# Between the layers of a graph network: the order of ScalarE's work over four chunks, and which queue issues the loads

## The chip, the cores and the metric

One core of a Trainium2 chip runs the whole kernel. The metric is the device time of one execution in microseconds (us); several runs are made and their median is given. Beside them one execution is recorded by the hardware profiler, and its trace is what the views below are read from.

The engines are called as in the profile: PE (TensorE matmul) with PEld (its weight loads), DVE (VectorE), ACT (ScalarE), POOL (GpSimd) and SP (SyncE). SP and ACT can both issue DMAs; "SPq" and "ACTq" mark that in the trace.

## The reference

Two layers of a graph network over 3125 nodes with 256 features and 50000 edges. Each layer adds a graph part and an attention part to `x`, and then a mixture-of-experts part:

```python
xn = _layernorm(x)
x = x + L0_gnn(xn, ...) + L0_mix(xn, ...)
x = x + L0_ffn(_layernorm(x), ...)          # shared expert + two of eight routed experts
xn = _layernorm(x)
x = x + L1_gnn(xn, ...) + L1_mix(xn, ...)   # attention over edges; Galerkin attention
x = x + L1_ffn(_layernorm(x), ...)

# L1_gnn, its start:
h_fwd = h @ W_forward.T                     # (3125, 64)
h_rev = h @ W_reverse.T
messages = h_fwd[src] * direction[:, 0:1] + h_rev[src] * direction[:, 1:2]
scores = messages @ attn.T                  # 4 heads
```

The change is in the step between the two layers: the two routed expert outputs of each node are added to `x`, `x` is normalised, transposed, and multiplied by the weights of `h_fwd` and `h_rev` and of the scores. The result is a table with one row of 136 values per node, from which the next step gathers by `src`.

## The kernel before

The 3125 nodes lie on 125 partitions in 25 tiles; `CHUNKS` groups the tiles as four chunks of four and three chunks of three. `self.x` stays in SBUF as 125 x 25 x 256 floats.

Layer 0's routed experts (`layer0_ffn`) scatter their outputs to `y2` in DRAM, two rows per node. When all scatters are done, `layer1_mix` calls `experts_in`, the function of the change. Its pools are closed when it ends; `layer1_mix` then takes new pools and fetches rows of `tab1` by indirect DMA on POOL (`gather`, L51), 391 of them in groups of eight, for the messages of layer 1. Layer 1's Galerkin attention is worked in between, and `layer1_ffn` follows.

`experts_in` runs in a block in which the order of PE, VectorE, ScalarE and SP is the order of the program (`manual_schedule`). In it:

- The loads: for each chunk, `y_in` (125 x 2 x 4 x 256) is read from `y2`, the first expert's half by SP, the second by ScalarE. `move` (L67) splits each half by partitions, 112 and 13, so there are 28 DMA issues, 14 on each of the two.
- `moments` (L1373 to L1378): VectorE adds both halves to `x`, takes `bn_stats` and `bn_aggr` of each tile; ScalarE takes the root of the variance.
- `table` (L1380 to L1400): VectorE takes the reciprocal (L1383) and minus mean times reciprocal (L1384). ScalarE writes the normalised rows (`ln_row`, L1388), one instruction per tile. PE transposes them (L1393) into PSUM (`ln_pt`, two halves of 128 features), and ScalarE copies them to `xT` (L1394). For each tile PE multiplies by `wcat` (`token_matmul`, L191) into a PSUM tile `pw`, and ScalarE copies it to `t1_st` (L1399), which the trace shows as `t_st`. SP stores the chunk to `tab1`, in two DMAs (L67), which the trace shows as `tab<-t_st`.
- The order: `moments` of a chunk, then `table` of the chunk before it.

Of the kernel before, what the change touches and what calls it, by code (L numbers as in the profile page):

```python
# [8 lines left out]
F32 = mybir.dt.float32  # L9
# [10 lines left out]
P = 125  # L20
NT = 25
CHUNKS = ((0, 4), (4, 4), (8, 4), (12, 4), (16, 3), (19, 3), (22, 3))
# [40 lines left out]
def move(queue, out, in_):  # L63


    for s in (slice(0, 112), slice(112, P)):
        queue.dma_start(out[s], in_[s])  # L67
# [7 lines left out]
def rows_of(table):  # L75
    return table.rearrange("(t p) d -> p t d", p=P)
# [12 lines left out]
class Kernel:  # L89
# [1265 lines left out]
    def experts_in(self, pool, psum, psum_m, xT):  # L1355

        nc, W = self.nc, 68
        mv = pool.tile([P, NT, 2], F32, name="ln_mv2")  # L1360
        rs = pool.tile([P, 2, NT], F32, name="ln_rs2")
        y2 = self.y2[:2 * N].rearrange("(i t p) d -> p i t d", i=2, p=P)
        loads = []
        for t0, n in CHUNKS:
            r = pool.tile([P, 2, 4, D], F32, name="y_in", bufs=len(CHUNKS))
            for i, queue in enumerate((nc.sync, nc.scalar)):
                move(queue, r[:, i, :n, :], y2[:, i, t0:t0 + n, :])
            loads.append(r)

        def moments(r, t0, n):  # L1370
            s = slice(t0, t0 + n)
            for i in range(2):
                nc.vector.tensor_add(self.x[:, s, :], self.x[:, s, :], r[:, i, :n, :])  # L1373
            st = pool.tile([P, 4, 6], F32, name="ln_st2", bufs=2)
            for t in range(t0, t0 + n):
                nc.vector.bn_stats(st[:, t - t0, :], self.x[:, t, :])
                nc.vector.bn_aggr(mv[:, t, :], st[:, t - t0, :])
            nc.scalar.activation(rs[:, 0, s], mv[:, s, 1], AF.Sqrt, bias=self.eps[:P])  # L1378

        def table(t0, n):  # L1380
            s = slice(t0, t0 + n)

            nc.vector.reciprocal(rs[:, 0, s], rs[:, 0, s])  # L1383
            nc.vector.scalar_tensor_tensor(rs[:, 1, s], mv[:, s, 0], -1.0, rs[:, 0, s], op0=OP.mult, op1=OP.mult)  # L1384
            row = pool.tile([P, 4, D], F32, name="ln_row2", bufs=2)
            for i in range(n):
                t = t0 + i
                nc.scalar.activation(row[:, i, :], self.x[:, t, :], AF.Identity, bias=rs[:, 1, t:t + 1],  # L1388
                                     scale=rs[:, 0, t:t + 1])
            for k in range(2):  # L1390
                pt = psum.tile([128, 4, P], F32, name="ln_pt")
                for i in range(n):
                    nc.tensor.transpose(pt[:, i, :], row[:, i, k * 128:(k + 1) * 128], self.ident[:P, :P])  # L1393
                nc.scalar.copy(xT[:, k, t0 * P:(t0 + n) * P], pt[:, :n, :].rearrange("p a b -> p (a b)"))  # L1394
            st = pool.tile([P, 4, 2 * W], F32, name="t1_st", bufs=2)
            for i in range(n):
                pm = psum_m.tile([P, 4, 65], F32, name="pw").rearrange("p h c -> p (h c)")[:, :2 * W]
                self.token_matmul(pm, xT, t0 + i, self.wcat)
                nc.scalar.copy(st[:, i, :], pm)  # L1399
            move(nc.sync, rows_of(self.tab1)[:, t0:t0 + n, :], st[:, :n, :])  # L1400

        before = None
        for r, chunk in zip(loads, CHUNKS):
            moments(r, *chunk)
            if before is not None:
                table(*before)
            before = chunk
        table(*before)

    def layer1_any_order(self):  # L1410

# [572 lines left out]
```

## Time and profile before

| What | us |
|---|---|
| median of 3 runs (2798.62 to 2800.9) | 2798.82 |
| the profiled execution, its own time | 2800.13 |
| its span in the trace | 2798.4 |
| first load of `y_in` issued (SP) | 1537.50 |
| first addition of `y_in` to `x` starts | 1544.11 |
| last of ScalarE's load issues begins | 1560.1 |
| first root begins | 1561.88 |
| last store of `tab1` issued | 1610.6 |
| first gather from `tab1` begins | 1613.86 |

Over the whole span PE is busy for 79%, POOL 59%, DVE 54% and ACT 19%. These shares say little on a stage of some 75 us out of 2800: the views that count are those restricted to the stage. In the table of busy time by stretch, each row gives the stretch, its length, the busy time of each engine with the number of its instructions in brackets, the granted PE clock (1.00 is full speed), the mean busy share of the DMA engines (it can exceed 1[...]) and GB/s. In a timeline, each row has the start, the length from the first start to the last end of a run of like instructions, what they are and how many; in square brackets stands how long the engine was idle before them, and what released it.

### The profile page before, as it was taken

The page shows a single profiled execution, that of the slowest core. Times are in us where ns is not written, and L with a number is a line of the kernel's source. Part 1 is how long each engine was busy: PE and PEld are TensorE (multiplying, and loading weights), DVE is VectorE, ACT ScalarE, POOL GpSimd, SP SyncE. Part 2 cuts the span into 40 slices and gives each one's busy share as a digit, 9 for nine tenths or more (in the row PEclk, how much of TensorE's full clock was granted, in tenths as well). Part 3 has the DMA queues.
Part 4 walks back from the last instruction along what each step waited for, and adds up shares of the span by engine and source line. Part 5 has one row for each costly group of instructions (what it writes and reads, how often), then busy time and mean ns, then how long its engine had stood idle before and what let it go on. Part 6 is the DMA issues. An engine that isn't in the chain of part 4 may idle for free. (4 is left out here: it accounts for less than half of the span.)

```text
span 2798.4 us, 26658 instructions
## 1 busy us (share of the span) xinstructions
PE 2201.9 (79%) x9047; PEld 1657.6 (59%) x9047; DVE 1508.4 (54%) x3589; ACT 544.0 (19%) x1116; POOL 1659.7 (59%) x1486
## 2 busy tenths in 40 slices
PE   1761659999976997999999549998667756999963
PEld 1551547876763665888887436665555644666642
DVE  7976499455568701222111459988658861222226
ACT  2320000000011111222222424444000020132213
POOL 4888788773002804666665077777747606777751
PEclk9955769999977998999999669999888867999976
DMA  8920433224400304455553421111211121112252
GB/s 296 382 102 14 116 90 90 62 52 90 114 32 21 81 5 160 163 184 181 183 189 107 113 70 49 47 47 47 57 32 41 39 66 40 25 40 53 53 109 70
DMA packets 175937, 259.79 MB, mean 93 GB/s; under 512 B 53839, under 2 KB 140857, under 8 KB 172402
## 3 DMA queue, kind: packets, MB, share of 16 engines
q1 hardware_dynamic: 114273, 198.43, 23.1%
q0 software_dynamic: 52288, 47.17, 7.3%
q10 hardware_dynamic: 9222, 12.30, 1.4%
q8 instruction: 76, 1.25, 0.2%
q14 instruction: 78, 0.64, 0.1%
HBM read 173.99 MB, written 83.69 MB: 92 GB/s over the span
## 5 line engine op out<-in xcount | busy, mean ns | idle before, releaser
L58 POOL DMA_INDIRECT adj<-ch_sum,ch_place x391 | 505.9, 1294 | 152.8 <-issue 109.7
L51 POOL DMA_INDIRECT g<-tab,t_src x391 | 459.0, 1174 | 152.6 <-issue 110.8
L58 POOL DMA_INDIRECT sorted<-s_rows,pos x256 | 245.1, 957 | 181.9 <-DVE s_rows L1059 112.4
L460 PE MATMUL psum<-sup,adjT 125*125 125x256 f32 x1250 | 294.1, 395 | 50.9 <-DMA adjT<-adj 39.6
L1288 PE MATMUL pw<-v,hot 128*125 128x260 f32 x1244 | 318.1, 417 | 0.0
L51 POOL DMA_INDIRECT G<-tabg,g_src x256 | 252.6, 987 | 80.2 <-issue 71.2
L460 PEld LDWEIGHTS psum<-sup,adjT 125*125 125x125 f32 x1250 | 241.8, 195 | 92.7 <-DMA adjT<-adj 36.4
L1288 PEld LDWEIGHTS pw<-v,hot 128*125 128x125 f32 x1244 | 252.2, 206 | 47.0
L866 PE MATMUL ph<-xs,w 128*128 128x256 f32 x960 | 219.3, 387 | 22.9 <-issue 20.5
L866 PEld LDWEIGHTS ph<-xs,w 128*128 128x128 f32 x960 | 183.2, 193 | 58.2 <-issue 31.0
L894 PE MATMUL py<-w,h 128*128 128x256 f32 x960 | 216.7, 379 | 0.0
L1700 PE MATMUL fpy<-fw,fh 128*125 128x256 f32 x800 | 186.2, 389 | 32.9 <-DVE y L1702 28.0
L1700 PEld LDWEIGHTS fpy<-fw,fh 128*125 128x125 f32 x800 | 152.6, 192 | 70.4 <-DVE y L1702 29.2
L894 PEld LDWEIGHTS py<-w,h 128*128 128x128 f32 x960 | 180.1, 190 | 23.3
L868 ACT ACTIVATE h<-ph,b 128x256 f32<-128x256 f32 x240 | 113.4, 473 | 361.4 <-PE ph L866 330.1
L1692 PE MATMUL fph<-xT,fw 128*128 128x500 f32 (+1 forms) x448 | 175.8, 542 | 0.2 <-DMA fw<-in_L_ffn_W_dram 0.2
L1034 PE MATMUL pctx<-s_mv,s_ro 128*128 128x256 f32 x512 | 155.4, 415 | 1.9 <-DVE s_mv L1033 1.9
L58 POOL DMA_INDIRECT slots<-rows,abi x50 | 74.3, 1485 | 100.2 <-DVE r_cum L948 85.3
L897 DVE TENSOR_SCALAR yo<-py,own 128x256 f32<-128x256 f32 x60 | 27.8, 481 | 190.8 <-PE py L894 190.8
L1694 ACT ACTIVATE fh<-fph,cols 128x500 f32<-128x500 f32 (+1 forms) x112 | 70.2, 632 | 298.0 <-PE fph L1692 264.0
L1692 PEld LDWEIGHTS fph<-xT,fw 128*128 128x128 f32 x448 | 85.4, 192 | 72.0 <-issue 49.4
L463 DVE TENSOR_TENSOR x<-x,psum 125x512 f32<-125x512 f32 (+1 forms) x104 | 68.9, 664 | 109.4 <-PE psum L460 109.3
(535 smaller groups left out, 3355.0 us busy)
## 6 DMA issues: line engine op xcount, KB each, us to landing
adjT<-adj SPq DMA_DIRECT2D x25, 1367.2 KB
adj<-zero SPq DMA_DIRECT2D x22, 1536.0 KB
w<-in_L_ffn_W1p_dram SPq DMA_DIRECT2D x30, 1024.0 KB
w<-in_L_ffn_W2p_dram SPq DMA_DIRECT2D x30, 1024.0 KB
slots<-empty SPq DMA_DIRECT2D x1, 8448.0 KB
srow<-slots SPq DMA_DIRECT2D x30, 264.0 KB
adj<-ch_sum,ch_place POOLq DMA_INDIRECT x391
g<-tab,t_src POOLq DMA_INDIRECT x391
```

The source lines that it names most:

```text
L51: nc.gpsimd.indirect_dma_start(out=out, out_offset=None, in_=table, in_offset=bass.IndirectOffsetOnAxis(ap=idx, axis=0))
L58: return nc.gpsimd.indirect_dma_start(out=table, out_offset=bass.IndirectOffsetOnAxis(ap=idx, axis=0), in_=rows, in_offset=None, **kw)
L460: nc.tensor.matmul(pm[:, i, :], mats[b][:, (a0 + i) * P:(a0 + i + 1) * P], sup[:, b, :], start=(b == b0), stop=(b == b0 + n - 1))
L463: nc.vector.tensor_add(xs, xs, pm[:, :m, :])
L866: nc.tensor.matmul(ph, w1[:, k, f * 128:(f + 1) * 128], xs[:, k, :], start=(k == 0), stop=(k == 1))
L868: nc.scalar.activation(h[:, f, :], ph, AF.Gelu, bias=b1[:, f:f + 1])
L894: nc.tensor.matmul(py, h[:, f, i * 128:(i + 1) * 128], w2[:, f, :], start=(f == 0), stop=(f == FC - 1))
L1034: nc.tensor.matmul(p1, ro[:, f - f0, :], mv, **st)
L1288: nc.tensor.matmul(pw.rearrange("p h c -> p (h c)"), hot[:, i - i0, :], v[:, i, :, :].rearrange("p h c -> p (h c)"), start=(i == i0), stop ...
L1692: nc.tensor.matmul(ph[:, :n * P], w1[:, k, f * 128:(f + 1) * 128], xT[:, k, t0 * P:(t0 + n) * P], start=(k == 0), stop=(k == 1))
L1694: nc.scalar.activation(hs[:, f, :n * P], ph[:, :n * P], AF.Gelu, bias=self.col("L1_ffn_b1", ei * FC + f))
L1700: nc.tensor.matmul(py, hs[:, f, i * P:(i + 1) * P], w2[:, f, :], start=(f == 0), stop=(f == FC - 1))
```

## The change

All 28 loads are issued by SP. `table` is split in three: `rows` (reciprocal, and the rows on ScalarE), `turned` (transposes on PE and their copies) and `table` (products and their copies, and the store). In turn c the program takes the moments and the root of chunk c, the rows of c-1, the transposes of c-2 and the products of c-3; three turns without moments end it. Two tiles of products share one PSUM tile (2 x 256 floats, of which 2 x 136 are used) and are copied by one instruction; a chunk of three tiles has a pair and a single. `t1_st` has three buffers in place of two; the PSUM pool of `pw` has four buffers, as before.

```diff
         for t0, n in CHUNKS:
             r = pool.tile([P, 2, 4, D], F32, name="y_in", bufs=len(CHUNKS))
-            for i, queue in enumerate((nc.sync, nc.scalar)):
-                move(queue, r[:, i, :n, :], y2[:, i, t0:t0 + n, :])
+            for i in range(2):
+                move(nc.sync, r[:, i, :n, :], y2[:, i, t0:t0 + n, :])
             loads.append(r)
...
-        def table(t0, n):
+        def rows(t0, n):
             s = slice(t0, t0 + n)
 
             nc.vector.reciprocal(rs[:, 0, s], rs[:, 0, s])
...
                 nc.scalar.activation(row[:, i, :], self.x[:, t, :], AF.Identity, bias=rs[:, 1, t:t + 1],
                                      scale=rs[:, 0, t:t + 1])
+            return row
+
+        def turned(row, t0, n):
             for k in range(2):
                 pt = psum.tile([128, 4, P], F32, name="ln_pt")
                 for i in range(n):
                     nc.tensor.transpose(pt[:, i, :], row[:, i, k * 128:(k + 1) * 128], self.ident[:P, :P])
                 nc.scalar.copy(xT[:, k, t0 * P:(t0 + n) * P], pt[:, :n, :].rearrange("p a b -> p (a b)"))
-            st = pool.tile([P, 4, 2 * W], F32, name="t1_st", bufs=2)
-            for i in range(n):
-                pm = psum_m.tile([P, 4, 65], F32, name="pw").rearrange("p h c -> p (h c)")[:, :2 * W]
-                self.token_matmul(pm, xT, t0 + i, self.wcat)
-                nc.scalar.copy(st[:, i, :], pm)
+
+        def table(t0, n):
+            st = pool.tile([P, 4, 2 * W], F32, name="t1_st", bufs=3)
+            for i in range(0, n, 2):
+                m = min(2, n - i)
+                pm = psum_m.tile([P, 2, 256], F32, name="pw")[:, :, :2 * W]
+                for j in range(m):
+                    self.token_matmul(pm[:, j, :], xT, t0 + i + j, self.wcat)
+                nc.scalar.copy(st[:, i:i + m, :], pm[:, :m, :])
             move(nc.sync, rows_of(self.tab1)[:, t0:t0 + n, :], st[:, :n, :])
 
-        before = None
-        for r, chunk in zip(loads, CHUNKS):
-            moments(r, *chunk)
-            if before is not None:
-                table(*before)
-            before = chunk
-        table(*before)
+
+        ready = {}
+        for c in range(len(CHUNKS) + 3):
+            if c < len(CHUNKS):
+                moments(loads[c], *CHUNKS[c])
+            if 0 <= c - 1 < len(CHUNKS):
+                ready[c - 1] = rows(*CHUNKS[c - 1])
+            if 0 <= c - 2 < len(CHUNKS):
+                turned(ready.pop(c - 2), *CHUNKS[c - 2])
+            if 0 <= c - 3 < len(CHUNKS):
+                table(*CHUNKS[c - 3])
```

## The prediction

> **What bounds the kernel now.** The diff touches one function, `experts_in`, so I first ask where in the span it lies and what it holds up. The list of waits for 1530 to 1615 us answers both (engine, tile or line waited at, releaser: us in total, times, longest).
>
> ```profile
> POOL late L1196 <- DMA tab<-t_st: 77.1, 1, 77.1
> ACT L1378 <- DMA y_in<-y: 39.1, 1, 39.1
> ...
> DVE ln_rs L1383 <- ACT ln_rs L1378: 23.0, 5, 8.7
> ...
> ACT t_st L1399 <- PE pw L191: 16.8, 25, 1.0
> ...
> DVE top L1204 <- DMA tab<-t_st: 13.9, 1, 13.9
> ```
>
> GpSimd does nothing for 77.1 us until the last store of `tab1` has landed; VectorE waits for the same store. PE, ScalarE and the SP queue start nothing of the next stage before it either (the timeline has the first next-stage load at 1612.73, the first gather at 1613.86). So this stage is serial with the rest: it runs from the first load, 1537.5, to 1612.8, and its 75.3 us are on the path. Nothing else is in flight, so a shorter stage moves all that follows. (The page's printed chain of waits starts only at 2269 us, which is why I use the waits.)
>
> Next the table of busy time by stretch shows what limits each part.
>
> ```profile
> core 0: us, PE busy (x) PEld busy (x) DVE busy (x) ACT busy (x) POOL busy (x), PEclk, DMA share, GB/s
> 1537.50:1544.10 6.60, 0.00 (x0) 0.00 (x0) 0.00 (x0) 0.00 (x0) 0.00 (x0) 0.50 0.86 204
> 1544.10:1553.50 9.40, 0.00 (x0) 0.00 (x0) 8.98 (x20) 0.00 (x0) 0.00 (x0) 0.50 1.12 255
> 1553.50:1562.20 8.70, 0.00 (x0) 0.00 (x0) 0.00 (x1) 1.60 (x3) 0.00 (x0) 0.50 1.07 254
> 1562.20:1576.00 13.80, 10.84 (x42) 8.15 (x43) 13.11 (x34) 7.97 (x19) 0.00 (x0) 0.62 0.21 54
> 1576.00:1610.20 34.20, 26.41 (x110) 20.52 (x109) 8.24 (x25) 19.38 (x51) 0.00 (x0) 0.70 0.14 36
> ```
>
> Three things: VectorE is full for two chunks and then stands still for 8.7 us; afterwards no engine is full, though each is often waited for; and loads fill the DMA engines at about 255 GB/s until 1564. The ScalarE timeline (start, us, what, idle before) gives the cause of the stop and the rhythm after it.
>
> ```profile
> 1537.74 22.82 ACTq L67 DMA_DIRECT2D y_in<-y  x14
> 1560.58 1.28 ACT L1378 ACT_TABLE_LOAD   x1 [39.05 <-DMA y_in<-y]
> 1561.88 0.48 ACT L1378 ACTIVATE ln_rs<-ln_mv,eps 125x4 f32<-125x4 f32 x2
> ...
> 1570.66 2.06 ACT L1388 ACTIVATE ln_row<-x,ln_rs 125x256 f32<-125x256 f32 x4
> 1573.14 1.05 ACT L1394 COPY xT<-ln_pt 128x500 f32<-128x500 f32 x2 [0.42 <-PE ln_pt L1393]
> 1575.09 0.27 ACT L1399 COPY t_st<-pw 125x136 f32<-125x136 f32 x1 [0.90 <-PE pw L191]
> 1576.00 0.27 ACT L1399 COPY t_st<-pw 125x136 f32<-125x136 f32 x1 [0.63 <-PE pw L191]
> 1576.91 0.27 ACT L1399 COPY t_st<-pw 125x136 f32<-125x136 f32 x1 [0.64 <-PE pw L191]
> 1577.81 0.27 ACT L1399 COPY t_st<-pw 125x136 f32<-125x136 f32 x1 [0.63 <-PE pw L191]
> 1577.98 0.30 ACT L1378 ACTIVATE ln_rs<-ln_mv,eps 125x4 f32<-125x4 f32 x1
> ```
>
> ScalarE issues 14 of the 28 loads, and the later ones go out only as earlier ones land: the last at about 1560.2. Both roots stood ready behind them (1548.8 and 1553.5). Then a chunk is one serial round: rows, PE transposes, copy, PE products, four copies each after its product, and only then the next root: 7.5 us for four tiles (1570.5 to 1578.0), 6.0 to 7.1 for three.
>
> **What the Trainium skill says.** "DMA: Bandwidth & Descriptors", Issuing engines are not separate DMA queues: issuing from several engines saves only issue time, the 16 DMA engines are shared. The trace agrees as far as it goes: the late layer's `yback` loads, of the same 1 KB rows and on SP alone (with a store and a few gathers beside them), run at 205 to 268 GB/s between 2702 and 2716 us. "TensorE: Matmul & The Clock Gate", Part 1: the clock is half until a window of about 3.4 us was busy, and falls back after idling. The trace agrees: PEclk is 0.50 before, 1.00 at 1572 to 1574 after PE was full from 1564 to 1570, and 0.57 in the next two microseconds although PE had been a half busy between. "ScalarE: Activation LUTs", What ACT_TABLE_LOAD costs: a copy without pointer operands takes 186 ns and 0.833 ns per element. The rows here are slightly below (272 ns at 136 columns, 299 by the page).
>
> **The change, part by part.** Durations are from this trace.
>
> *Loads.* ScalarE loses 14 issues; SP gains 14 of 0.3 to 0.4 us. SP's 28 issues (some 10 us) fit in the 22 us over which the transfers meter them out; eight were in flight over both queues at first (four on each), and the SP-only `yback` loads got about eight out too. Chunk 0's four issues are now in series, so it may land 0.4 us later. Behind them SP has the stores of `tab1`, the first needed near 1568, after the last load issue near 1560: nothing is delayed. The root of chunk 0 no longer waits for 1560.5, so VectorE's 8.7 us stop goes.
>
> *VectorE is then the pacer.* Its order is unchanged. Moments take 4.66 us for four tiles (1562.50 to 1567.16) and 3.68 for three; reciprocal and product 0.28 a chunk. From 1544.1: 4 x 4.66 + 3 x 3.68 + 6 x 0.28 = 31.4, so the last moments end at 1575.5. Loads keep ahead: chunks 1 to 6 are 5.38 MB, at 205 GB/s 26.2 us, thus in by 1570.3, before VectorE reaches the last chunk at 1571.8.
>
> *ScalarE, staggered.* In one turn it does root c, rows c-1, copies c-2, table copies c-3, so PE has a turn to get ready. Pitches: root 0.2, rows 4 x 0.52, transposed copies 2 x 0.53. The 25 single copies (0.272 each) become 14, of which 11 have two tiles: from 272 ns at 136, 474 at 375 and 578 at 500 columns I estimate 0.39 us at 272 (0.41 by the page), pitch 0.32. Four tiles: 0.2 + 2.1 + 1.06 + 0.64 = 4.0 us a turn, below VectorE's 4.94. Added wait: a root waits for its moments with the rows and copies of three older chunks queued behind it, and PE's products and SP's stores wait for those. It costs nothing while VectorE paces the turns; its price is the three turns that remain at the end.
>
> *PE.* A cold tile of products takes 0.90 us (spacing of the copies), a warm one 0.46 (1591.65 to 1592.11); a transpose 0.24 or 0.12 when rows are ready. Four tiles: 5.5 us cold, 2.8 warm. Cold it is slower than VectorE, then full, and full is what makes it warm; so I expect alternation, with little lag.
>
> *Tail, warm.* At 1575.5 ScalarE owes root 6 (0.3), rows 5 (1.57), copies 4 (0.87), table 3 (0.64), rows 6 (1.57), copies 5 (0.87), table 4 (0.52), copies 6 (0.87), table 5 (0.52): 7.7 us; then the last product and copy, 1.2: about 1584.4. *Cold throughout*, PE sets the end: from the first transpose of chunk 1 (1559.4), 21 tiles x 2 x 0.24 + 25 x 0.90 = 32.6, plus about 1.2 of waits and the last copy: 1593.2. I take a quarter of the way, 1586.6, plus 0.4 for the first landing: 1587.0. Today the last copy ends at 1610.2; store and landing after it (2.6 us) stay. **Gain 23.2 us.**
>
> *Third `t1_st` buffer, four pair-wide PSUM tiles:* nothing; a pair is copied only when both its tiles are done, which the one-turn delay covers. Without that cover it is one tile, 0.46 to 0.90 us, per pair.
>
> **Sum.** The profiled execution took 2800.13 us (span 2798.4), 1.3 above the median of 2798.82. The gain is a difference within the trace and carries over to the median: 2798.8 - 23.2 = 2775.6.
>
> **Rivals.**
> *PE stays cold* (0.15). For it: before, PE is at half clock most of the time. Against: it then is 100% busy. End 1593.6, gain 16.6: 2782.
> *One queue is slower* (0.10): if loads only reach 150 GB/s, 5.38 MB take 35.9 us, the last chunk lands at 1580.4, its moments end at 1584.1, tail 9: 1593.1 and up; at 120 GB/s 1601.9. Some 2782 to 2791. Against: the `yback` rate.
> *The gain is given back* (0.04): gathers after 1613.9 take another course, or the clock of later PE stages falls otherwise; within 0.2% of today, 2793 to 2804. Against: all engines start the next stage together from idle.
> *Slower* (0.05): one SP ring starves the DMA engines. The point from which it decides: last landing past 1597.5 (1610.2 less 9 and 3.7), that is 5.38 MB in 53.0 us, 101 GB/s. At 90 GB/s the last copy falls at 1617.0: 2805.6. For it: twice the issues share one queue, and each waits for an earlier transfer.
> That the order is not kept is no case: this block is scheduled by hand for PE, VectorE, ScalarE and SP.
>
> **How the numbers follow.** My forecast has 0.66; its own span is 2771 (warm, first landing not late, 1 us of run spread) to 2780. The range goes on through the cold case and the milder slow-queue case: 2769 to 2787. A measurement of this kernel tells about 0.2% (5.6 us) from no change. Faster: 0.66 + 0.15 + 0.10 = 0.91; same 0.04; slower 0.05.
>
> **What would show it.** Right: the first root near 1550, no stop of VectorE above 1 us between 1544 and 1575, rows of chunk 0 before 1555, 14 table copies of which 11 are near 0.39 us, last copy at 1584 to 1590, first gather 23 us earlier. Wrong: y_in below 200 GB/s, VectorE waiting for loads, PEclk at 0.50 through 1590 (the cold case), or a message stage longer than its 1613.9 to 2265.7.

## The result, and the profile after

The changed kernel takes **2772.03 us** (median of 6 runs, 2770.59 to 2775.72) against 2798.75 (6 runs of the kernel before): 26.7 us less, ratio **0.9909**, 95% interval 0.9896 to 0.9923. The forecast was 2775.6, with a gain of 23.2. The profiled execution of the changed kernel took 2771.34 us, with a span of 2769.6.

The two spans differ by 28.8 us. Cut at the first load issue of the stage, the start of GpSimd's next work (when the last store of `tab1` has landed) and the first load of the last layer, they compare so:

| Part of the span | before, us | after, us | difference |
|---|---|---|---|
| up to the first `y_in` issue | 1537.5 | 1535.4 | -2.1 |
| the stage of the change | 75.3 | 47.3 | **-28.0** |
| messages of layer 1 | 652.9 | 653.9 | +1.0 |
| last layer | 532.7 | 532.9 | +0.2 |

The 2.1 us ahead of the stage are not the change's, since the two kernels are the same up to there. The stage gain was passed on but for 1.2 us, which leaves 26.8, close to the 26.7 of the medians. The waits of the stage (engine, tile and line waited at, releaser: us in total, times, longest) show what went:

```profile
POOL late L1196 <- DMA tab<-t_st: 49.1, 1, 49.1
ACT L1378 <- DVE ln_mv L1377: 26.1, 1, 26.1
PE ln_pt L1396 <- ACT ln_row L1388: 22.2, 8, 19.1
...
ACT ln_rs L1378 <- DVE ln_mv L1377: 7.6, 4, 2.9
...
ACT t_st L1406 <- PE pw L191: 0.7, 1, 0.7
```

ScalarE's first root now waits for VectorE's moments and no longer for loads; VectorE's 23.0 us of waiting for roots is gone from the list; ScalarE's 16.8 us of waiting for products has become 0.7. The stretches (length, busy time of each engine, PE clock, DMA share, GB/s):

```profile
1535.44:1541.89 6.45, 0.00 (x0) 0.00 (x0) 1.23 (x2) 0.00 (x0) 0.00 (x0) 0.50 0.87 212
1541.89:1550.31 8.42, 0.00 (x0) 0.00 (x0) 8.01 (x22) 1.84 (x3) 0.00 (x0) 0.50 1.12 246
1550.31:1561.90 11.59, 8.64 (x31) 6.28 (x32) 11.08 (x26) 7.33 (x17) 0.00 (x0) 0.50 1.05 254
1561.90:1571.40 9.50, 8.74 (x66) 7.59 (x66) 8.95 (x28) 9.06 (x22) 0.00 (x0) 0.98 0.24 62
1571.40:1580.20 8.80, 7.89 (x57) 6.42 (x56) 0.59 (x5) 7.89 (x21) 0.00 (x0) 1.00 0.38 99
```

VectorE is full from 1541.9 to the last moments at 1571.4 (28.0 of 29.5 us). In the tail after that PE and ScalarE are both busy for 7.9 of 8.8 us. PE's clock is at full speed from just after 1562. The ScalarE timeline has the turn that was intended, here with the rows of chunk 3, the copies of 2, and the table copies of 1 with no wait in between:

```profile
1563.75 0.30 ACT L1378 ACTIVATE ln_rs<-ln_mv,eps 125x3 f32<-125x3 f32 x1
1564.07 2.08 ACT L1388 ACTIVATE ln_row<-x,ln_rs 125x256 f32<-125x256 f32 x4
1566.05 1.03 ACT L1397 COPY xT<-ln_pt 128x500 f32<-128x500 f32 x2
1566.97 0.67 ACT L1406 COPY t_st<-pw 125x272 f32<-125x272 f32 x2
1567.61 0.30 ACT L1378 ACTIVATE ln_rs<-ln_mv,eps 125x3 f32<-125x3 f32 x1
```

### The profile page after: what moved, and what is told of

Read it like the earlier page. It is cut to its first block, busy times and chain, and to the rows that moved or that the text cites. A ratio compares the mean times of both kernels' runs of the same rounds, so it can differ in the third digit from the quotient of the medians.

```text
span 2769.6 us, 26648 instructions
## 1 busy us (share of the span) xinstructions
PE 2190.7 (79%) x9047; PEld 1650.7 (60%) x9047; DVE 1506.8 (54%) x3589; ACT 541.6 (20%) x1105; POOL 1661.3 (60%) x1486
```

## The experiments

They ran on other chips of the same kind, where the kernel before takes 3176 to 3206 us. The changed kernel has a stage of 47.8 us on such a chip (`e11`, in the last group), so for it the excess lies outside the stage. Each kernel is therefore read by the length of its stage in its own trace, one execution each (first `y_in` issue to GpSimd's first instruction after the last landing), and by the ratio of its time to that of the kernel before on the same chip. The kernel before left no trace there: its 75.3 us are from the first chip. `e5`, `e6`, `e7` and `e9` ran once each, so only their stages are used.

**The parts, singly and in pairs.** `e1` is the kernel before with this edit alone:

```diff
-            for i, queue in enumerate((nc.sync, nc.scalar)):
-                move(queue, r[:, i, :n, :], y2[:, i, t0:t0 + n, :])
+            for i in range(2):
+                move(nc.sync, r[:, i, :n, :], y2[:, i, t0:t0 + n, :])
```

> The kernel before with only the first part of the change: SP issues all 28 loads; one round per chunk and single copies stay. The stage (first load issue to the landing of the last table store, seen at GpSimd's first instruction) was 75.3 us before and 47.3 after. Theory A (a root stood behind ScalarE's own blocked issues, worth VectorE's 8.7 us stop, and chunk 0 lands earlier from one queue, 1.3): stage 65.3 us (64 to 67), time about 2789. Rival B (issuing queues only save issue time, so the order of ScalarE's work makes the gain): stage 74 to 75, time 2798. Rival C (one queue feeds slower): y_in below 230 GB/s and VectorE waiting for loads after chunk 0.

Measured: stage 62.3 us, 13.0 less; ratio 0.9975 (0.9945 to 1.0005), so whole runs alone do not tell this gain. Theory A has the cause right, but the stage lies below its range: ScalarE's waits for products fell too, from 16.8 to 13.9 us. Rival C falls: VectorE does not wait for loads after chunk 0.

`e2` is the changed kernel with the two queues put back:

```diff
-            for i in range(2):
-                move(nc.sync, r[:, i, :n, :], y2[:, i, t0:t0 + n, :])
+            for i, queue in enumerate((nc.sync, nc.scalar)):
+                move(queue, r[:, i, :n, :], y2[:, i, t0:t0 + n, :])
```

> The changed kernel with the loads as before, half of them issued by ScalarE; the staggered turns and the pair copies stay. Theory A: the roots stand behind the issues until about 23 us into the stage, VectorE stops again for 8 to 9 us, then 2 x 4.9 + 3 x 3.9 us of moments follow, 8.8 of tail and 2.6 of landing: stage 57.8 us (57 to 60), time about 2782. Rival B (the order alone carries the gain): stage 47 to 49, time 2772.

Measured: stage 58.6 us, ratio 0.995 (0.9925 to 0.9975). The ScalarE timeline shows the stop again: issuing for 23.8 us, then the table load, then two roots at once.

```profile
1798.52 23.80 ACTq L67 DMA_DIRECT2D y_in<-y  x14
1822.36 1.28 ACT L1378 ACT_TABLE_LOAD   x1 [40.04 <-DMA y_in<-y]
1823.65 0.48 ACT L1378 ACTIVATE ln_rs<-ln_mv,eps 125x4 f32<-125x4 f32 x2
```

This is in the range of theory A. Rival B falls with both runs: the loads are worth 13.0 us without the new order and 11.3 with it, the order 16.7 without the loads and 15.0 with them.

`e3` keeps loads and turns, but copies each tile of products alone:

```diff
-            for i in range(0, n, 2):
-                m = min(2, n - i)
-                pm = psum_m.tile([P, 2, 256], F32, name="pw")[:, :, :2 * W]
...
+            for i in range(n):
+                pm = psum_m.tile([P, 4, 65], F32, name="pw").rearrange("p h c -> p (h c)")[:, :2 * W]
+                self.token_matmul(pm, xT, t0 + i, self.wcat)
+                nc.scalar.copy(st[:, i, :], pm)
```

> The changed kernel with one copy per tile of products and the old PSUM tile, so 25 copies of 136 columns in place of 14; loads on SP and staggered turns stay. Theory A: the pairs save ScalarE 25 x 0.18 less 14 x 0.3, some 1 us over the stage, and only that of the last three turns is on the path: stage 47.3 to 48.5. Rival D (with four single PSUM tiles ScalarE waits for each product again, as before): 0.2 to 0.5 us for each of 25 tiles, stage 52 to 58.

Measured: stage 47.6 us, ratio 0.9922 (0.9894 to 0.995). ScalarE waits 0.6 us for products in all. Pairs are not what took the waits away; the delay is.

`e4` is `e1` with the pairs:

```diff
-            for i in range(n):
-                pm = psum_m.tile([P, 4, 65], F32, name="pw").rearrange("p h c -> p (h c)")[:, :2 * W]
-                self.token_matmul(pm, xT, t0 + i, self.wcat)
-                nc.scalar.copy(st[:, i, :], pm)
+            for i in range(0, n, 2):
+                m = min(2, n - i)
+                pm = psum_m.tile([P, 2, 256], F32, name="pw")[:, :, :2 * W]
...
```

> The kernel before with the loads on SP and the pair copies, but one serial round per chunk. Theory A: in a serial round a pair waits for both of its products and saves one copy; stage as with the loads alone, within 1 us (64 to 67). Rival D: the pairs are what takes the waits for products away: stage 55 to 60.

Measured: stage 66.0 us, ratio 1.0 (0.998 to 1.002). Rival D falls. Theory A's 64 to 67 holds the number, but not its claim: it is **3.7 us more** than with the loads alone, not within 1. Without the delay a pair waits for its second product, as its waits show (14 copies, 18.6 us, against 25 copies and 13.9 in `e1`), in the timeline mostly 1.8 us at the first pair:

```profile
1809.99 0.39 ACT L1401 COPY t_st<-pw 125x272 f32<-125x272 f32 x1 [1.81 <-PE pw L191]
```

PE's clock is lower too: its mean is 0.67 over the second half of the rounds, against 0.86 in `e1`, and for the same 150 instructions PE is busy for 38.4 us in place of 33.6. How much of the 3.7 us is the clock's, these runs do not tell; it could be all of it.

**Issuing, or being blocked.** `e5` gives ScalarE 4 of the 28 issues:

```diff
             for i in range(2):
-                move(nc.sync, r[:, i, :n, :], y2[:, i, t0:t0 + n, :])
+                queue = nc.scalar if i and t0 < 8 else nc.sync
+                move(queue, r[:, i, :n, :], y2[:, i, t0:t0 + n, :])
```

> The changed kernel, but ScalarE issues the second half of the first two chunks (4 of 28 issues), SP the rest. These four go out while nothing has to land first. Theory A (it is the blocked issues that cost, not the issuing): ScalarE is free about 2 us into the stage, no stop of VectorE between chunks. The first half of chunk 0 shares the engines with its second half again, so VectorE starts at 6.5 us in place of 4.5 and the stage is 48.6 (48 to 49.5). Rival (any issue by ScalarE delays the roots): stage 55 or more. Rival (the early landing has nothing to do with the second queue): VectorE starts at 4.5, stage 47.3.

Measured: stage 49.1 us. VectorE begins 6.9 us after the first issue (1789.10) and then waits for no root. ScalarE's four issues are over 2.3 us after it, and the first root waits for its moments alone:

```profile
1789.34 2.10 ACTq L67 DMA_DIRECT2D y_in<-y  x4
...
1800.81 0.30 ACT L1379 ACTIVATE ln_rs<-ln_mv,eps 125x4 f32<-125x4 f32 x1 [8.06 <-DVE ln_mv L1378]
```

So four issues by ScalarE are cheap; in the kernel before, standing behind issues that wait for earlier landings is what cost. And the second queue does delay the first half of chunk 0: VectorE began after 4.5 us in the changed kernel and after 4.7 in `e11`. The stage is 1.3 to 1.8 us longer.

**Is PE the pacer?** `e6` works each product twice:

```diff
-                    self.token_matmul(pm[:, j, :], xT, t0 + i + j, self.wcat)
+                    for _ in range(2):
+                        self.token_matmul(pm[:, j, :], xT, t0 + i + j, self.wcat)
```

> The changed kernel with each tile of products worked twice into the same PSUM region, the second overwriting the first: 25 x 0.48 = 12 us more of warm PE. Theory A (VectorE paces until its last moments, PE is warm with 40% to spare, the tail is exposed): PE then needs 4.8 us of 4.9 in a turn of four, the turns stay, and only the products left at the last moments (13 tiles) show, 6.2 us: stage 53 to 56. Rival (PE paces the stage): the full 12 us and more, stage 59 to 61, with VectorE stopping.

Measured: stage 55.0 us, within the range of theory A. The last moments end 36.5 us after the first issue; in the changed kernel they do at 36.0, and at 36.4 in `e11`. VectorE stops only after them, for 2.0 us. So of the 12 us of added products none to speak of show while VectorE paced, and 7.2 us in the tail and landing (18.5 us against 11.3).

**One turn of delay less.** `e7`:

```diff
-        for c in range(len(CHUNKS) + 3):
+        for c in range(len(CHUNKS) + 2):
...
-            if 0 <= c - 3 < len(CHUNKS):
-                table(*CHUNKS[c - 3])
+            if 0 <= c - 2 < len(CHUNKS):
+                table(*CHUNKS[c - 2])
```

> The changed kernel with the products of c-2 in the turn of its transposes, so one turn of delay less. Theory A (the delay keeps ScalarE from waiting on PE): ScalarE waits for the first product and again for the second pair, 1.5 to 2 us a turn, a turn becomes 5.5 to 6 us against VectorE's 4.9, and the saved last turn does not make up for it: stage 51 to 58. Rival (the third turn only lengthens the tail): stage 44.5 to 46.

Measured: stage 59.4 us, just beyond the range of theory A; the rival falls. The list of waits shows a wait in both directions:

```profile
ACT t_st L1406 <- PE pw L191: 14.0, 11, 1.8
PE pw L191 <- ACT xT L1397: 13.9, 7, 4.1
```

In the same turn PE needs ScalarE's copies and ScalarE needs PE's products, so each idles while the other works. PE's clock has a mean of 0.66 between 1858 and 1880. But over the whole stage, here of `e7` and of the changed kernel, its mean is the same, and PE is busy for only 1.1 us more:

```profile
1842.57:1901.97 59.40, 26.41 (x150) 23.16 (x150) 30.09 (x78) 26.48 (x61) 0.00 (x0) 0.72 0.60 137
1535.44:1582.76 47.32, 25.27 (x150) 20.30 (x150) 29.86 (x78) 26.13 (x61) 0.00 (x0) 0.72 0.72 172
```

So PE hardly worked longer; its work is no longer hidden. The third turn is worth 12 us.

**The tail, and a version that beats both?** `e9` moves the rows and transposed copies of the last chunk to VectorE:

```diff
+                if t0 == CHUNKS[-1][0]:
+                    nc.vector.tensor_scalar(row[:, i, :], self.x[:, t, :], rs[:, 0, t:t + 1], rs[:, 1, t:t + 1],
+                                            op0=OP.mult, op1=OP.add)
...
-                nc.scalar.copy(xT[:, k, t0 * P:(t0 + n) * P], pt[:, :n, :].rearrange("p a b -> p (a b)"))
+                copy = nc.vector.tensor_copy if t0 == CHUNKS[-1][0] else nc.scalar.copy
+                copy(xT[:, k, t0 * P:(t0 + n) * P], pt[:, :n, :].rearrange("p a b -> p (a b)"))
```

> The changed kernel with the rows and the two transposed copies of the last chunk on VectorE, which has nothing left to do after the last moments. Theory A (the tail is ScalarE's queue): 2.4 us less on ScalarE, up to 1 us of it given back to waits for PE: stage 45 to 46.5. Rival (the tail is the chain through PE, whatever ScalarE does): stage 47.3 within 0.5.

Measured: stage 46.7 us, a gain of 0.6 to 1.0, less than theory A held. The timeline says where the rest went:

```profile
1825.07 1.06 DVE L1389 TENSOR_SCALAR ln_row<-x,ln_rs 125x256 f32<-125x256 f32 x3
...
1826.94 1.55 PE L191 MATMUL pw<-wcat,xT 128*125 128x136 f32 x12
...
1828.33 0.81 PE L1400 MATMUL ln_pt<-ident,ln_row 125*128 125x125 f32 x6
```

The rows are ready at 1826.1, but PE's order has chunk 4's products ahead of chunk 6's transposes, and they begin at 1828.3. The tail depends on PE's order too, not on ScalarE's queue alone.

`e8` puts the first addition on GpSimd, `e10` is that with `e9`, and `e11` is the changed kernel again:

```diff
-            for i in range(2):
-                nc.vector.tensor_add(self.x[:, s, :], self.x[:, s, :], r[:, i, :n, :])
+            nc.gpsimd.tensor_add(self.x[:, s, :], self.x[:, s, :], r[:, 0, :n, :])
+            nc.vector.tensor_add(self.x[:, s, :], self.x[:, s, :], r[:, 1, :n, :])
```

> The changed kernel with the first of the two additions of y_in to x on GpSimd, which stands idle in this stage. Theory A (VectorE paces the turns until its last moments): a turn of four on VectorE falls from 4.9 to 3.7 us, then loads (4.1 us a chunk) and ScalarE (4.0) pace; last moments end at about 30 us in place of 35.9, stage 42 to 44. It holds if GpSimd adds 1024 columns in under about 4 us; no run so far shows such an addition. Rival (GpSimd is slower than the 4.9 us it relieves, or slows VectorE beside it): stage over 47.3, VectorE waiting for x from GpSimd. Rival (ScalarE paces already): stage 46.5 to 47.3.

> The kernel with the first addition on GpSimd, and the rows and transposed copies of the last chunk on VectorE. Theory A: as with the addition alone, and 0.6 us less as when the last chunk alone was moved (46.7 against 47.3): stage 41 to 43. Rival: as that run, within 0.3.

> The changed kernel itself, beside the kernel before on this chip. Stage 47.3 within 0.5, gain of the whole 27 us within the noise of this chip's runs.

Measured: stages of 45.8, 45.3 and 47.8 us; ratios to the kernel before 0.988 (0.9847 to 0.9912), 0.9903 (0.9869 to 0.9937) and 0.9901 (0.9868 to 0.9933). The gain of 2.0 to 2.4 us in the stage is below what whole runs can tell here, so no version is shown to beat the changed kernel. `e8` missed its range by 1.8 us. `e10` missed its own by 2.3: the last chunk on VectorE brought 0.5 us, as much as two executions of the changed kernel differ by (47.3 and 47.8). Lines of `e8`:

```profile
1793.70 2.34 POOL L1372 TENSOR_TENSOR x<-x,y_in 125x1024 f32<-125x1024 f32 x1 [6.57 <-DMA y_in<-y]
...
1816.88 2.06 ACT L1388 ACTIVATE ln_row<-x,ln_rs 125x256 f32<-125x256 f32 x4
1818.85 1.03 ACT L1397 COPY xT<-ln_pt 128x500 f32<-128x500 f32 x2
1819.78 0.67 ACT L1406 COPY t_st<-pw 125x272 f32<-125x272 f32 x2
```

GpSimd needs 2.34 us where VectorE needs 1.22, which puts the first root 0.7 us later; and from 1812.7 on ScalarE goes from one instruction to the next without a wait, until the last pair. With VectorE relieved, ScalarE paces.

`e12` therefore relieves both: chunk 0 is added on VectorE, and VectorE takes one of the two transposed copies of each chunk.

```diff
             for i in range(2):
-                nc.vector.tensor_add(self.x[:, s, :], self.x[:, s, :], r[:, i, :n, :])
+                add = nc.gpsimd.tensor_add if t0 and not i else nc.vector.tensor_add
+                add(self.x[:, s, :], self.x[:, s, :], r[:, i, :n, :])
...
-                nc.scalar.copy(xT[:, k, t0 * P:(t0 + n) * P], pt[:, :n, :].rearrange("p a b -> p (a b)"))
+                copy = nc.vector.tensor_copy if k else nc.scalar.copy
+                copy(xT[:, k, t0 * P:(t0 + n) * P], pt[:, :n, :].rearrange("p a b -> p (a b)"))
```

> The changed kernel with the first addition of chunks 1 to 6 on GpSimd (chunk 0 keeps both on VectorE, since GpSimd's 2.34 us against 1.22 delayed the first root), and one of the two transposed copies of each chunk on VectorE. Theory A as amended (with VectorE relieved, ScalarE's 4.0 us a turn and its queue in the tail pace; it must be relieved too): ScalarE 3.5, VectorE 4.2, loads 4.1 a turn of four; last moments near 31 us, tail 6.5 to 7.5, landing 2.6: stage 40 to 42. Rival (what is left is the chain of three turns of delay, whoever works it): stage 44.5 to 46.

Measured: stage 46.7 us, ratio 0.9938 (0.9914 to 0.9963); the amended theory missed by 5 us. The last moments end at 36.0 us, as in the changed kernel, for VectorE was not relieved: it is busy for 29.5 us of the stage, against 29.9. Its timeline has two reasons:

```profile
1811.46 0.75 DVE L1385 SCALAR_TENSOR_TENSOR ln_rs<-ln_mv,ln_rs 125x4 f32<-125x4 f32 x1
1812.13 0.67 DVE L1399 COPY xT<-ln_pt 128x500 f32<-128x500 f32 x1
...
1816.95 1.99 DVE L1374 TENSOR_TENSOR x<-x,y_in 125x768 f32<-125x768 f32 x1
```

The copy costs it 0.67 us a chunk of four, and while GpSimd adds, an instruction of VectorE that takes 0.16 us elsewhere takes 0.75 here, and one addition 1.99 in place of 0.95. Once, at chunk 1, it also stood for 1.4 us until GpSimd had added. What was taken from VectorE came back as a copy and as waiting on GpSimd.

The times say how. In `e8`, `e10` and `e12` nine of these small instructions, which read two tensors, began while GpSimd added; each ended 0.01 to 0.03 us after GpSimd's addition did. The longest is in `e10`:

```profile
1800.17 2.34 POOL L1372 TENSOR_TENSOR x<-x,y_in 125x1024 f32<-125x1024 f32 x1 [2.66 <-DMA y_in<-y]
1801.13 1.40 DVE L1384 SCALAR_TENSOR_TENSOR ln_rs<-ln_mv,ln_rs 125x4 f32<-125x4 f32 x1
```

`bn_stats`, which reads one tensor, took its usual 0.39 us beside such an addition. The other way round, GpSimd's additions of 768 columns took 1.82 us, and 2.14 to 2.16 in the three cases that began while VectorE added. That each waits for the other is read from these times; no run tests it apart.

## Why the prediction was right

**The stage is serial, and its gain passes on whole.** Right: 28.0 us off the stage, of which 1.2 came back behind it.

**ScalarE's blocked issues hold up the roots.** Right, by `e1`, `e2` and `e5`. The first two roots came when their moments did (the first after the 1.28 us table load), and VectorE's 8.7 us stop was gone. "DMA: Bandwidth & Descriptors", Issuing engines are not separate DMA queues, holds for the transfers (254 GB/s from SP alone), but the saving named there, the issue time, is not what ScalarE got back: its compute had stood behind issues that waited for landings.

**Chunk 0 lands 0.4 us later.** Wrong in sign; this is a term mis-sized by 1.7 us. Two lines of VectorE's timeline after:

```profile
1539.96 1.23 DVE L1373 TENSOR_TENSOR x<-x,y_in 125x1024 f32<-125x1024 f32 x1 [7.53 <-DMA y_in<-y]
1541.89 1.23 DVE L1373 TENSOR_TENSOR x<-x,y_in 125x1024 f32<-125x1024 f32 x1 [0.70 <-DMA y_in<-y]
```

From one queue the first half is there 4.5 us after the first issue and the second at 6.45; from two queues the first addition began at 6.6. So the first addition hides behind the second half's landing, and the first moments end 9.9 us into the stage; the forecast had 11.7. `e5` shows the late start again with a second queue.

**VectorE paces at 31.4 us from there.** Right as a mechanism, 0.6 us too long: five pairs of reciprocal and product stand before the last moments and not six (0.28), and each of the three turns of three took 3.86 us and not 3.96.

**PE is cold for a quarter of the way.** The step that failed most: 2.2 us were added for it, and none were needed. The sum for a warm PE gave 8.9 us from the last moments to the last copy, and 8.7 were measured. The reason given (a cold PE is full, and full is what makes it warm) held: the clock rose just after 1562, when PE had been full since 1556, and stayed at 1.00 until the stage's end. "TensorE: Matmul & The Clock Gate", Part 1, agrees with that as it did with the kernel before; the mistake was to discount it. `e6` adds that PE is not the pacer before the tail.

**Pairs and a third buffer at nothing; 0.39 us a pair copy.** Right for the pairs: 0.390 us measured for 11 of them, and a stage of 47.6 us without pairs against 47.3 and 47.8 with them. The third buffer was not tested apart. The price without cover, one tile a pair or 0.46 to 0.90 us, was above what showed in the end: 3.7 us over 11 pairs is 0.34 (`e4`), with the copies saved already taken off and a lower clock in it.

**Store and landing 2.6 us.** Right: 1580.17 to 1582.76.

The terms together: 23.2 forecast, plus 2.2 (PE), 1.7 (first landing), 0.6 (VectorE) and 0.2 (tail) is 27.9, against 28.0 in the trace. Within the stage these errors all point the same way, so none hid another. Of the signs of being right, the last copy (1580.2) and the first gather (30 us earlier) came sooner than named, of which 2.1 us are the earlier start of the stage; of those of being wrong only one came, and by 1.0 us, the longer message stage.

The rivals: the slow queue falls (254 GB/s); the cold PE falls (clock 1.00 through the tail); the slower case needed 101 GB/s; the gain given back was at most 1.2 us in the trace.

## What to carry to other kernels

An engine that computes should not issue DMAs that have to wait for earlier ones to land: here 14 such issues held ScalarE for 22.8 us, and 4 that did not have to wait held it for 2.1. The cost is not the issue but what stands behind it in the engine's order, and it is read where an engine's DMA issues stretch over the whole of the transfers. Where two engines answer each other within one round, give each partner a turn of time by working on older chunks in between; batching their hand-over without that delay made this stage 3.7 us slower, in part perhaps by the clock. Price the next pacer before relieving the present one: here relieving VectorE, ScalarE's last chunk or both took at most 2.4 us off the stage.

## What the runs showed of the hardware

- With the halves of chunk 0 on two queues, VectorE could begin 6.6 us (kernel before) or 6.9 us (`e5`) after the first issue, with both on one queue 4.5 and 4.7 us (changed kernel and `e11`), at about the same total rate, 255 and 254 GB/s.
- A fp32 addition of 1024 columns on 125 partitions took 2.34 us on GpSimd and 1.22 on VectorE. VectorE instructions of 0.16 us that read two tensors and began beside such an addition ended with it, and so took up to 1.40; `bn_stats` was not slowed.
- The same program took 13 to 15% longer on other chips (the kernel before 3176 to 3206 us against 2799), while this stage kept its length (47.3 and 47.8 us in the changed kernel). There the time up to the stage was 1790.5 us in place of 1535.4; what makes it was not studied.
